# Three of the seven products of the last matrix product split once more, from the second block on

## The chip, the cores and the metric

The kernel runs on one core of one Trainium2 chip. The metric is device microseconds from start to end of one execution. The kernel before takes 3126.12 us (median of three runs, 3125.75 to 3136.84).

## What is computed

The input is x, 4 batches of 2048 tokens with 512 channels, fp32. With xn = layernorm(x) the result is

```
xr, xk, xv = mixes of xn and of xn one token earlier, weights mu_r, mu_k, mu_v
r, k, v    = xr Wr^T, xk Wk^T, xv Wv^T                      (512 -> 512 each)
wkv        = the RWKV-v4 recurrence over tokens, per channel, on k and v
attn       = (sigmoid(r) * wkv) Wo^T                        (512 -> 512)
hidden     = fwht(silu(xn W1^T) * (xn W3^T))                (512 -> 2048)
out        = x + attn + hidden W2^T                         (2048 -> 512)
```

fwht is a fixed orthogonal transform of the 2048 hidden channels; the kernel folds it into W2 once, at its start. The last two products are then one: 2048 hidden rows and 512 rows of sigmoid(r)*wkv, together 2560 rows, are multiplied by one matrix with 512 output columns.

## The kernel before, in words

All tensors have channels on the 128 partitions and tokens along the free dimension. The tokens are cut into 8 blocks of 1024 (`TB`), two to a batch. Every block passes through three stages.

1. **Projections** (k, v, r in this order). From block 1 on each is done by `projected_pair` (line 365), six units in all, `n` = 0 to 5.
2. **Up** (W1 and W3), 16 units of `up` (line 396). Between their instructions `step()` issues, piece by piece, the recurrence `wkv` on VectorE and ScalarE.
3. **Down**, the last product (`down`, line 496), 2560 rows into 512 columns. While it runs, the chores of the next block are issued (`next_tokens`, line 689): its tokens are loaded, their layernorm statistics taken (`statistics`, line 134), the input normalised (`normalize`, line 145), mixed (`mixed`) and combined (`mix_forms`).

All three stages use a scheme with seven instead of eight products (Strassen's, in Winograd's order). The right side (rows x 1024 tokens) is cut into four quarters: two halves of the rows and two halves of 512 tokens; the weights into four quarters alike. Sums of weight quarters are made once and kept in DRAM (`part_w` for projections and up, `down_w` for down), seven forms per weight. Sums of the right-hand quarters are made on VectorE or GpSimd as they are needed, and the seven products are added up partly in PSUM, partly by copies on ScalarE and additions on VectorE. In `down` one of the seven products is 10 row tiles (`NR`) for each of two groups `g` of 128 output channels: 20 matmuls of 128x128 weights by 512 tokens. Seven products are 140 matmuls. The right-hand quarters are named y11, y12, y21, y22 there; `difference` overwrites them in place as the products no longer need their old content.

**Order.** `InOrder` (line 24) keeps the instructions of every engine in the order in which the program issues them. All DMAs are issued by one queue, SyncE's (SP). An instruction there that waits (a store for the addition that fills its source, say) holds everything behind it.

**Weights.** Those of projections and up come in units of 896 KB through a ring of three buffers (`ring_a`, `load_parts`, line 349), two units ahead. The first two units of the next block are loaded by `next_parts` (line 709), which `down` calls as `w_after` ahead of its seventh product:

```
            if k == 6:
                w_after()
            elif k:
                w.append(load_down(i, order[k + 1]))
```

The weights of `down` come as whole forms of 1280 KB (`load_down`, line 483) into `ring_b`, two buffers. The four stage buffers (`stage`, line 96) and `x22_of` hold the residual x, take the sums, and are stored to `outT` from there. `x_tok` (the next block's tokens) lies in `k_sb`, whose content the recurrence has used up by then.

Of the kernel before, what the change touches and what calls it, by code (L numbers as in the profile page):

```python
# [14 lines left out]
P = 128  # L15
# [24 lines left out]
def tile_rwkv_attn_hadamard_ffn(  # L40
# [20 lines left out]
    NR = (NF + NB) // 2  # L61
    n_blocks = NT // TB
# [6 lines left out]
    ring_b = ctx.enter_context(tc.tile_pool(name="ring_b", bufs=2))  # L69
# [6 lines left out]
    down_w = dram.tile([7, P, NR, KH, P], F32, name="down_w")  # L76
# [3 lines left out]
    hid = const.tile([P, NF, TB], F32, name="hid")  # L80
    xnT = const.tile([P, NB, OFF + TB], F32, name="xnT")
    tf = const.tile([P, 4, KH, H], F32, name="tf")
    r_sb, k_sb, v_sb = (const.tile([P, NB, TB], F32, name=n) for n in ("r_sb", "k_sb", "v_sb"))
# [3 lines left out]
    turn = [0]  # L87

# [11 lines left out]
    mix_of[2], mix_of[0] = hid[:, 0:NB, :], hid[:, NB : 2 * NB, :]  # L100
    t4_of = {kind: hid[:, NF // 2 + n, :] for n, kind in enumerate((1, 2, 0))}
# [43 lines left out]
    def normalize():  # L145
        for b in range(NB):
            eng = dve if b < KH else pool
            for s, op in ((0, ALU.mult), (1, ALU.add)):
                xb = xnT[:, b, OFF : OFF + TB]
                eng.tensor_tensor(xb, xb, spread[:, s, :], op)  # L150
# [52 lines left out]
    def load_square(i, kind):  # L203
        t = ring_b.tile([P, NB, C], F32, tag="b", name=f"w_{i}_{kind}")
        sp.dma_start(out=t, in_=wrkv[kind])
        return t

    def projected(kind, w, h, half):
        pt = bank()
        for b in range(NB):  # L210
            pe.matmul(
                pt, lhsT=w[:, b, ts(h, P)], rhs=mix_of[kind][:, b, ts(half, H)], start=(b == 0), stop=(b == NB - 1)
            )
        dst = (r_sb, k_sb, v_sb)[kind][:, h, ts(half, H)]
        if kind == 0:
            act.activation(dst, pt, AF.Tanh, scale=0.5)
        else:
            act.copy(dst, pt)


    def wkv(h):
        w_h, u_h = weff[:, h : h + 1], vec[:, 4, h : h + 1]
        r, k, v = r_sb[:, h, :], k_sb[:, h, :], v_sb[:, h, :]
# [67 lines left out]
    def mix_forms(kind):  # L291

        m11, m12, m21, m22 = quarters(mix_of[kind], 0)
        if kind == 1:
            f1, f2 = (by_tile(s[:, OFF : OFF + TB]) for s in (sa, sb))
        else:
            slot = ring_b.tile([P, 2, KH, H], F32, tag="b", name=f"mf_{kind}")
            f1, f2 = slot[:, 0], slot[:, 1]
        f4 = by_tile(t4_of[kind])
        right_of[kind] = (m11, m21, m22, f1, f2, m12, f4)  # L300
        for out, x, y in ((f1, m12, m11), (f2, m22, f1), (m12, m22, m12), (f4, m21, f2)):
            dve.tensor_tensor(out, x, y, ALU.subtract)
            yield
# [61 lines left out]
    def projected_pair(i, n, w, tail, hook):  # L365
# [3 lines left out]
        dst = (r_sb, k_sb, v_sb)[kind]  # L369
        d11, d12, d21, d22 = (dst[:, mh * KH + g, ts(t, H)] for mh in range(2) for t in range(2))  # L370
# [25 lines left out]
    def up(i, j, w, tail, step):  # L396

        keep_parts(i, 3 * KH + j, w)
        h0, h1 = hid[:, j, 0:H], hid[:, j, H:TB]
# [24 lines left out]
    NP = NF // 2  # L424
    fold = [hid[:, NP + n, :] for n in range(NP)]

# [37 lines left out]
    def down_parts(n):  # L464
        t = ring_b.tile([P, 7, KH, P], F32, tag="b", name=f"df_{n}")
        if n >= NP:
            sp.dma_start(out=t[:, 0:4], in_=wo[n - NP])
        return t

    def down_forms(j, at, t):  # L470
        n, a = at[j] if j < NP else (j, None)
        far = down_w[:, :, n].rearrange("f p k c -> p f k c")
        if n < NP:
            a = a.rearrange("p (k m g c) -> p k m g c", k=2, m=2, c=P)
            seven_forms([t[:, f] for f in range(4)], a[:, 0, 0], a[:, 1, 0], a[:, 1, 1], a[:, 0, 1])
            sp.dma_start(out=far[:, 0], in_=a[:, 0, 0])
            sp.dma_start(out=far[:, 1:3], in_=a[:, 1])
            sp.dma_start(out=far[:, 3:7], in_=t[:, 0:4])
        else:
            forms_in(t)  # L480
            sp.dma_start(out=far, in_=t)

    def load_down(i, form):
        t = ring_b.tile([P, NR, KH, P], F32, tag="b", name=f"dw_{i}_{form}")
        sp.dma_start(out=t, in_=down_w[form])
        return t

    def rows(kh, half):

        n = NF // 2  # L490
        pieces = [hid[:, kh * n + 2 * a : kh * n + 2 * a + 2, ts(half, H)] for a in range(n // 2)]
        return pieces + [r_sb[:, kh * KH : (kh + 1) * KH, ts(half, H)]]

    order = (0, 1, 4, 6, 5, 3, 2)

    def down(i, w, between, w_after, last):
        y11, y12, y21, y22 = rows(0, 0), rows(0, 1), rows(1, 0), rows(1, 1)
        def product(k, pts, right, start, then):
            if k == 6:
                w_after()  # L500
            elif k:
                w.append(load_down(i, order[k + 1]))
            if k:
                next(between)
            for g in range(KH):
                whole = slice(0, H)
                for pt, cols in ending if last and k == 6 and g == KH - 1 else [(pts[g], whole)]:
                    for n in range(NR):
                        pe.matmul(
                            pt[:, cols], lhsT=w[k][:, n, g, :], rhs=right[n // 2][:, n % 2, cols],  # L510
                            start=start and n == 0, stop=n == NR - 1, skip_group_check=True,
                        )
                    then(g) if cols == whole else c21(g, pt, cols)

        def difference(out, x0, x1):
            for o, p0, p1 in zip(out, x0, x1):
                dve.tensor_tensor(o, p0, p1, ALU.subtract)

        def at(mh, g, half):
            return ts(mh * KH + g, P), ds(i * TB + half * H, H)  # L520

        def residual(slot, mh, g, half):
            c, t = at(mh, g, half)
            sp.dma_start(out=slot, in_=xT[c, t])

        def store(slot, mh, g, half):
            c, t = at(mh, g, half)
            sp.dma_start(out=outT[c, t], in_=slot)

        add = dve.tensor_tensor  # L530
        pa, pb, pc = ([bank() for _ in range(KH)] for _ in range(3))
        ending = [(pb[KH - 1], slice(0, H // 2)), (bank(), slice(H // 2, H))]
        s5 = [small.tile([P, H], F32, tag="s5", name=f"s5_{i}_d{g}") for g in range(KH)]
        for g in range(KH):
            residual(stage[g], 0, g, 0)
        product(0, pa, y11, True, lambda g: act.copy(pb[g], pa[g]))
        difference(y11, y12, y11)

        def c11(g):
            add(stage[g], pa[g], stage[g], ALU.add)  # L540
            store(stage[g], 0, g, 0)
            residual(stage[2 + g], 0, g, 1)
            residual(x22_of[g], 1, g, 1)

        product(1, pa, y21, False, c11)
        product(2, pc, y11, True, lambda g: act.copy(s5[g], pc[g]))
        difference(y12, y22, y12)
        for g in range(KH):
            add(x22_of[g], x22_of[g], s5[g], ALU.add)
        product(3, pc, y22, False, lambda g: None)  # L550
        difference(y22, y22, y11)

        def u2(g):
            act.copy(u2_of[g], pb[g])

        product(4, pb, y22, False, u2)
        difference(y21, y21, y22)
        for g in range(KH):
            add(u2_of[g], u2_of[g], stage[2 + g], ALU.add)
            add(stage[2 + g], pc[g], u2_of[g], ALU.add)  # L560
            store(stage[2 + g], 0, g, 1)
            residual(stage[g], 1, g, 0)

        def c22(g):
            add(x22_of[g], pb[g], x22_of[g], ALU.add)
            store(x22_of[g], 1, g, 1)
            if last and g == KH - 1:
                act.copy(ending[1][0][:, H // 2 :], pb[g][:, H // 2 :])

        product(5, pb, y12, False, c22)  # L570

        def c21(g, pt=None, cols=slice(0, H)):
            add(stage[g][:, cols], (pb[g] if pt is None else pt)[:, cols], stage[g][:, cols], ALU.add)
            c, t = at(1, g, 0)
            sp.dma_start(out=outT[c, t][:, cols], in_=stage[g][:, cols])

        product(6, pb, y21, False, c21)
# [29 lines left out]
    for i in range(n_blocks):  # L607
# [64 lines left out]
        w_down = []  # L672
        for j in range(NF):
# [6 lines left out]
            if j >= NF - 2:  # L680
                w_down.append(load_down(i, order[j - NF + 2]))
# [7 lines left out]
        def next_tokens():  # L689
# [4 lines left out]
            normalize()  # L694
            yield
            mixed(1)
            yield
            pending[1] = mix_forms(1)
            for _ in range(3):
                next(pending[1])  # L700
            yield
            yield
            mixed(2)
            pending[2] = mix_forms(2)
            for _ in range(3):
                next(pending[2])
            yield

        def next_parts():
            if not last:  # L710
                parts.extend(load_parts(i + 1, n) for n in range(2))
# [3 lines left out]
        down(i, w_down, (None for _ in range(6)) if last else next_tokens(), next_parts, last)  # L715
# [53 lines left out]
```

## Time and profile before

| | |
|---|---|
| profiled execution, its own time | 3126.89 us |
| its span, first to last instruction | 3125.1 us |
| TensorE matmul busy | 3108.2 us (99%), 7252 records |
| VectorE busy | 2197.2 us (70%) |
| ScalarE busy | 873.9 us (28%) |
| GpSimd busy | 322.6 us (10%) |
| mean granted TensorE clock | 0.999 |
| DMA | 334.45 MB, mean 107 GB/s |

An fp32 matmul is recorded as two matmuls, each with its weight load, so 7252 records are 3626 matmuls of the program. Block 3, as an example, has its projections from 1200 us, its up stage to 1463.3 us and its down stage from 1463.28 to 1583.45 us. The down stage's busy times there (1463 to 1583 us) are 120.0 us TensorE, 66.65 us VectorE, 12.02 us ScalarE and 13.70 us GpSimd.

### The profile page before, as it was taken

The numbers are of one execution on the slowest core, as the hardware profiler recorded it, in microseconds if no ns is written. First come the engines' busy times: TensorE is split into PE (matmuls) and PEld (weight loads), VectorE is DVE, ScalarE is ACT, GpSimd is POOL, SyncE is SP. The second block draws the span as 40 slices with busy tenths as digits, with TensorE's granted clock in tenths as the row PEclk, the third lists the DMA queues.
The fourth block names the chain that finished last, engine by engine and source line by source line (L and its number), as shares of the span: only waits on it lengthen the run. The fifth ranks groups of instructions, "written<-read, shape, count | busy, mean of one in ns | idle before, by whom it ended". The sixth has DMA issues, their size and how long they took to land.

```text
span 3125.1 us, 20283 instructions
## 1 busy us (share of the span) xinstructions
PE 3108.2 (99%) x7252; PEld 1378.9 (44%) x7252; DVE 2197.2 (70%) x2317; ACT 873.9 (28%) x1375; POOL 322.6 (10%) x203
## 2 busy tenths in 40 slices
PE   8999999999999999999999999999999999999999
PEld 3444444444444444444444444444444444444444
DVE  6798847876478765797557965589564886658852
ACT  4233023330233203332123321333213331133310
POOL 3353131001100011000110001100011000010000
PEclk9999999999999999999999999999999999999999
DMA  4354433223322242222422233222332224322222
GB/s 163 104 183 162 161 116 110 77 109 135 108 77 76 103 153 96 76 78 107 150 93 78 75 133 123 97 75 79 136 135 78 79 74 160 111 84 73 80 97 78
DMA packets 75813, 334.45 MB, mean 107 GB/s; under 512 B 9152, under 2 KB 18624, under 8 KB 66368
## 3 DMA queue, kind: packets, MB, share of 16 engines
q1 hardware_dynamic: 75712, 333.15, 30.3%
q8 instruction: 58, 0.95, 0.1%
q14 instruction: 43, 0.35, 0.0%
HBM read 286.93 MB, written 46.19 MB: 107 GB/s over the span
## 4 chain that ended last, share of the span: by engine, by line
PE 99%; DVE 0%; DMA 0%; SPq 0%; issue 0%; ACT 0%; ACTq 0%
PE bank L34 99%; DVE xnT L34 0%; DMA hid<-w 0%; DVE tf L34 0%; SPq L34 0%; ACT tf L34 0%; ACT hid L34 0%; DVE v_sb L34 0%; ACTq L34 0%; ACT k_sb L34 0%
## 5 line engine op out<-in xcount | busy, mean ns | idle before, releaser
L34 PE MATMUL bank<-tf,part 128*128 128x512 f32 x2272 | 1042.2, 592 | 0.0
L34 PE MATMUL bank<-hid,dw 128*128 128x512 f32 (+1 forms) x1808 | 787.5, 588 | 0.0
L34 PE MATMUL bank<-xnT,part 128*128 128x512 f32 x1536 | 721.8, 592 | 0.0
L34 PEld LDWEIGHTS bank<-tf,part 128*128 128x128 f32 x2272 | 431.7, 190 | 543.4 <-issue 513.5
L34 ACT COPY bank<-bank 128x512 f32<-128x512 f32 x527 | 300.2, 570 | 1268.1 <-PE bank L34 1243.9
L34 PEld LDWEIGHTS bank<-hid,dw 128*128 128x128 f32 x1808 | 343.5, 190 | 426.0 <-issue 422.8
L34 PEld LDWEIGHTS bank<-xnT,part 128*128 128x128 f32 x1536 | 291.8, 190 | 367.4 <-issue 363.1
L34 DVE TENSOR_TENSOR hid<-hid 128x1024 f32<-128x1024 f32 (+1 forms) x173 | 221.8, 1310 | 105.2 <-PE bank L34 104.3
L34 DVE SCALAR_TENSOR_TENSOR hid<-hid,bank 128x512 f32<-128x512 f32 x256 | 174.0, 680 | 170.8 <-ACT hid L34 170.6
L34 PE MATMUL bank<-hid,part 128*128 128x512 f32 x616 | 271.2, 592 | 0.0
L34 DVE RECIPROCAL e1b<-e1b 128x512 f32<-128x512 f32 x64 | 214.1, 3347 | 1.1
L34 PE MATMUL bank<-r_sb,dw 128*128 128x512 f32 (+1 forms) x452 | 210.7, 588 | 0.0
L34 DVE TENSOR_TENSOR bank<-bank,s 128x512 f32<-128x512 f32 x256 | 168.0, 690 | 36.5 <-ACT bank L34 25.3
L34 ACT ACTIVATE hid<-bank 128x512 f32<-128x512 f32 x272 | 162.2, 600 | 94.0 <-PE bank L34 75.9
L34 PEld LDWEIGHTS bank<-hid,part 128*128 128x128 f32 x616 | 117.0, 190 | 147.3 <-issue 145.7
L34 DVE TENSOR_TENSOR hid<-hid,bank 128x512 f32<-128x512 f32 x256 | 173.6, 678 | 11.5 <-PE bank L34 7.1
L34 POOL TENSOR_TENSOR rs<-rs,neg_half 128x8 f32<-128x8 f32 x7 | 11.5, 1648 | 1581.1 <-DVE rs L34 1581.1
L34 DVE SCALAR_TENSOR_TENSOR hid<-xnT,vec,hid 128x1024 f32<-128x1024 f32 x64 | 93.1, 1489 | 97.2 <-ACT hid L34 97.2
L34 PEld LDWEIGHTS bank<-r_sb,dw 128*128 128x128 f32 x452 | 85.9, 190 | 106.4 <-issue 106.2
L34 ACT COPY s<-bank 128x512 f32<-128x512 f32 x128 | 75.0, 586 | 145.9 <-PE bank L34 145.9
L34 DVE TENSOR_TENSOR v_sb<-bank,v_sb 128x512 f32<-128x512 f32 (+1 forms) x33 | 22.1, 672 | 129.9 <-PE bank L34 129.9
L34 POOL TENSOR_TENSOR tf<-xnT 128x1024 f32<-128x1024 f32 x16 | 46.4, 2902 | 589.9 <-PE bank L34 589.9
(103 smaller groups left out, 2218.0 us busy)
## 6 DMA issues: line engine op xcount, KB each, us to landing
part<-part_w SPq DMA_DIRECT2D x148, 896.0 KB, 4.6
dw<-down_w SPq DMA_DIRECT2D x56, 1280.0 KB, 6.1
part_w<-part SPq DMA_DIRECT2D x22, 896.0 KB, 6.9
k_sb<-x SPq DMA_DIRECT2D x7, 2048.0 KB, 8.3
xnT<-xT SPq DMA_DIRECT2D x7, 2048.0 KB, 9.7
v_sb<-xT SPq DMA_DIRECT2D x48, 256.0 KB, 4.8
out<-v_sb SPq DMA_DIRECT2D x47, 256.0 KB, 2.1
part<-wpart SPq DMA_DIRECT2D x22, 512.0 KB, 5.0
```

Source lines behind the costliest of these rows:

```text
L34: return self.tc.keep_in_program_order(issue(*args, **kwargs))
```

## The change

Block 0 keeps the 140 matmuls of its down stage. From block 1 on, the products with forms 1, 4 and 6 (on y21, y11 and y22) are each split once more by the same scheme: their 10 row tiles into two halves of 5 (`QR`), their two channel groups, and their 512 tokens into two halves of 256. Such a product becomes seven products of 5 matmuls by 256 tokens, 35 in place of 20 by 512 tokens. The other four products stay.

- **Weights in pieces.** `pieces_w` holds eight pieces of 5 x 128 x 128 (320 KB). Every product of 5 matmuls has its own piece, loaded by `load_piece` seven products ahead. The extra weight forms are made once, in block 1's up stage on GpSimd (`deep_forms`, `keep_deep`, DRAM tensor `deep_w`). `pieces_w` also takes the place of the former `ring_b`. `down_w` has a new layout.
- **Right side.** `hid` and `r_sb` become one tensor `right`, so that five row tiles lie at one stride. The sums for the deep products (`Deep.forms`) are made on VectorE; they lie in the three buffers of `ring_a`, in `k_sb` and in `tf`. Differences are made by quarters of 5 x 256 elements (`differences`, `parts_of`).
- **PSUM and output.** A deep product clears half banks (`clear`, ScalarE), copies half banks within itself (`step`, ScalarE), and its two banks are added into the stage buffers (`onto`, VectorE).
- **Chores.** `next_tokens` is cut into 23 steps, handed out by `advance(n)` at other places; `normalize` runs wholly on VectorE instead of half on GpSimd.
- **First units of the next block.** `load_parts(i + 1, 0)` and `(i + 1, 1)` are now issued after `down` has returned.

The core of the diff:

```diff
-    ring_b = ctx.enter_context(tc.tile_pool(name="ring_b", bufs=2))
-    hid = const.tile([P, NF, TB], F32, name="hid")
+    right = const.tile([P, 2, NR, TB], F32, name="right")
+    pieces_w = const.tile([P, 8, QR, P], F32, name="pieces_w")
     def normalize():
         for b in range(NB):
-            eng = dve if b < KH else pool
             for s, op in ((0, ALU.mult), (1, ALU.add)):
                 xb = xnT[:, b, OFF : OFF + TB]
-                eng.tensor_tensor(xb, xb, spread[:, s, :], op)
+                dve.tensor_tensor(xb, xb, spread[:, s, :], op)
+                yield
...
+    program = [p1[0], p1[1], *deep(0, 0, 1), p1[2], *deep(0, 2), p1[3], *deep(0, 3, 4, 5), *deep(1, 0), *deep(0, 6)]
+    for m, n in ((1, 1), (2, 0), (1, 2), (2, 1), (1, 3), (1, 4), (2, 2), (1, 5), (2, 3), (2, 4), (2, 5), (1, 6), (2, 6)):
+        program += deep(m, n)
+    program += plain(5) + plain(3) + plain(2)
+    def piece(i, u):
+        return pieces_w[:, (u + 4 - len(program if i else whole_program)) % 8]
...
+        def product(self, pt, rows, cols, start=False):
+            load_piece(self.i, self.u + 7)
+            self.u += 1
+            self.matmuls(pt, self.u - 1, rows, cols, start)
...
+    class Deep:
+        def forms(self, *which):
+            q11, q12, q21, q22 = self.q
+            t1, t2, t3, t4 = self.t
+            for n in which:
+                difference(*((t1, q12, q11), (t2, q22, t1), (t3, q22, q12), (t4, q21, t2))[n])
+        def step(self, *which):
+            for n in which:
+                pt, rows, cols = (
+                    (a, q11, lo), (f, t1, lo), (b, t2, hi), (a, q22, hi), (a, q21, lo), (b, t3, hi), (b, t4, lo),
+                )[n]
+                self.down.product(pt, rows, cols)
+                if n == 0:
+                    act.copy(b[:, hi], a[:, lo])
+                elif n == 1:
+                    act.copy(self.s5, f[:, lo])
+                elif n == 2:
+                    act.copy(a[:, hi], b[:, hi])
+                elif n == 5:
+                    act.copy(b[:, lo], b[:, hi])
...
+    def down(i, advance, last):
+        d0.forms(0, 1, 2, 3)
+        plain_step(0, 0)
+        plain_step(0, 1)
+        d1.clear()
+        add(x11[0], pa[0])
+        advance(1)
+        d0.step(0, 1)
+        plain_step(1, 0)
+        differences(y11[0:2], y12[0:2], y11[0:2])
+        d1.forms(0)
+        d0.step(2)
+        differences(y12[0:2], y22[0:2], y12[0:2])
+        plain_step(1, 1)
+        add(x11[1], pa[1])
+        differences(y11[2:4], y12[2:4], y11[2:4])
+        d1.forms(1)
+        d0.step(3, 4)
+        d0.onto(x11, 0)
+        d1.forms(2, 3)
+        d0.step(5)
+        d1.step(0)
+        d0.step(6)
+        differences(y12[2:4], y22[2:4], y12[2:4])
+        d2.forms(0)
+        d0.onto(x11, 1)
+        d2.clear()
+        d2.forms(1)
+        d1.step(1)
+        d2.step(0)
+        d2.forms(2, 3)
+        d1.step(2)
+        d2.step(1)
...
+        d.plain_product(pa, (1, 1), c12)
+        d.residual(x21, 1, 0)
+        differences(y21, y21, y22)
+        d.plain_product(pa, (0, 1), c22)
+        advance(7)
+        if not last:
+            d.plain_product(pa, (1, 0), c21)
+            return
...
-        def next_parts():
-            if not last:
-                parts.extend(load_parts(i + 1, n) for n in range(2))
-
         if not last:
             load_tokens(i + 1)
-        down(i, w_down, (None for _ in range(6)) if last else next_tokens(), next_parts, last)
+        if i == 0:
+            down_whole(i, advance)
+        else:
+            down(i, advance, last)
+        if not last:
+            parts.extend(load_parts(i + 1, n) for n in range(2))
```

`c21(g)` adds the last sum into a stage buffer and stores it to `outT`; it is called after each half of the last product.

## The prediction, made before the changed kernel had run

> **What bounds the kernel now.** I read the list of waits first: no engine's wait on TensorE (PE) matters if PE itself never waits. Then the chain that ended last, the groups by form for the price of a matmul, and the timeline around one block boundary. The chain:
>
> ```profile
> 8.86 5.58 PE bank L34 x8
> ...
> 21.73 17.43 PE bank L34 x36
> ...
> 45.20 3076.61 PE bank L34 x7188
> 3121.81 0.02 issue
> 3121.83 0.42 DVE v_sb L34
> ```
>
> From 45 us on the chain is PE alone: its matmuls stand back to back, across the block boundaries too. So only two things count: how long PE needs, and whether the change makes it wait.
>
> The price of a matmul of each width, from the timeline of the ending, where the old kernel already has 256 columns (two records are one fp32 matmul):
>
> ```profile
> 3113.00 3.62 PE L34 MATMUL bank<-hid,dw 128*128 128x256 f32 x16
> 3116.45 1.03 PE L34 MATMUL bank<-r_sb,dw 128*128 128x256 f32 x4
> 3117.31 3.62 PE L34 MATMUL bank<-hid,dw 128*128 128x256 f32 x16
> ```
>
> 20 records from 3113.00 to 3117.31 are 0.2155 us each, 0.431 us a matmul. Of 512 columns, the 280 records of block 3's down stage (1463.28 to 1583.45) are 0.4292 each, 0.858 a matmul. Half the width costs half the time, with a weight load (190 ns) for each record.
>
> The boundary between block 3 and 4, from the timeline:
>
> ```profile
> 1567.58 0.92 SPq L34 DMA_DIRECT2D part<-part_w  x2
> 1576.11 8.60 SPq L34 DMA_DIRECT2D out<-v_sb  x2
> 1583.45 1.88 PE L34 MATMUL bank<-tf,part 128*128 128x512 f32 x4
> 1583.65 0.69 DVE L34 TENSOR_TENSOR v_sb<-bank,v_sb 128x512 f32<-128x512 f32 x1 [7.57 <-PE bank L34]
> 1584.76 0.42 SPq L34 DMA_DIRECT2D part<-part_w  x1
> ```
>
> PE goes over to the next block at 1583.45 without a gap, because that block's first two weight units were issued at 1567.58, before the last two stores. Those stores held SP's queue for 8.6 us, until the addition that PE's last matmul released (1583.65).
>
> **1. Fewer PE microseconds.** A deep product is 35 x 0.431 = 15.09 us in place of 20 x 0.858 = 17.16. Three a block, seven blocks: 420 matmuls of 512 columns go (360.4 us), 735 of 256 come (316.8): **-43.6 us**, 6.2 a block. The end of the last block was in halves before, so nothing changes there.
>
> **2. The block's first weights, moved behind the last store.** In the changed program unit 0 of the next block is issued by SP after both stores of c21, and the next block's first matmul waits for it. From PE's last matmul at T: the addition starts at T+0.20, ends at T+0.89, and SP gets to the unit at T+1.31 (1584.76 - 1583.45). Units (896 KB) land 4.0 us after issue at the least, 4.6 as the median; the three that were issued as the first of two took 4.7 to 5.4. Here three go out in a row, so I take 5.0. The first wait in the trace went from landing (8.73) to matmul in 0.14. PE idles 1.31 + 5.0 + 0.14 = **6.4 us** (5.4 to 6.9). Unit 1 lands some 2 us later and is needed 12 us later. Block 1's first units are the 512 KB kind, landing in 5.0, whose forms GpSimd makes at 0.99 each while PE has raw quarters: the same gap.
>
> An idle PE also loses its clock. At 17.86 us it stopped for 3.87 us:
>
> ```profile
> 14.27 3.60 PE L34 MATMUL bank<-hid,had_sb 128*128 128x512 f32 x8
> 21.73 12.26 PE L34 MATMUL bank<-tf,w 128*128 128x512 f32 x24 [3.87 <-ACT hid L34]
> ```
>
> The next PE row starts at 33.83: 24 records took 12.10 us, at 0.429 they are 10.30. The stop cost **1.8 us** more, and single records between 23.3 and 25 us show 1061 ns against 592. I take 1.8 for a gap of 6.4 us as well; the ends are 0 (the stop of 0.86 us at 44.3 shows no slow records) and 3.6, twice the row, since the gap is longer.
>
> The Trainium skill ("TensorE: Matmul & The Clock Gate", Part 1) states that an idle window of 3.4 us halves the clock until a busy window has passed, the windows running free. By that rule I estimate one to two half-speed windows, 1.7 to 3.4 us a boundary, and an end of 3139 to 3151.
>
> Seven boundaries: 7 x (6.4 + 1.8) = **+57.4 us**. What hid these loads before is the whole seventh product, 17 us; the change keeps no cover.
>
> **3. VectorE (DVE) in the down stage.** Rows: 1024 elements in a run of subtractions 4.62/4 = 1.155 us, so a quarter of 1280 is 1.44; an addition from PSUM 0.69, of 256 columns 0.43. With t from the stage's first matmul, DVE is free at 2.2 (1465.5 - 1463.28, its last up additions). The four d0 sums end at 8.0; the first addition follows PE's tenth matmul, 8.8 to 9.5; the statistics take 7.5 as before (1481.81 to 1489.3, GpSimd's power in them) and end at 17.2. Then DVE is solid work: 3 quarters and 2 of y12 to 24.6, an addition to 25.3, 3 quarters to 29.6, d0's first output (1.15) to 30.8, 5 quarters (d1's last two sums, two of y12, d2's first sum) to 38.0. PE wants d1's first operand at 30.1 (ready 18.9), d1's second sum at 38.7 (ready 29.6), d2's first sum at 40.9 (ready 38.0), y22 at 62.4 (ready 57.6, behind PE's reading), y21 at 96.7 (ready 86.3). Smallest slack **2.8 us**: nothing on the path. The added work, 12 sums (17 us) and about 6 us of additions a block, fits: DVE was busy 66.65 of 120 us there. Block 0 keeps its products; its y22 quarters are ready 1.2 us ahead.
>
> Normalising on DVE: the 1024-element rows are 1.22 alone and 2.98 while GpSimd works beside it. Three such steps at 49.9 and five at 64 leave y22 in time even at 2.98 (ready 61.7). They cost nothing; if DVE were late, each would cost its length.
>
> **4. Weights in pieces.** 37 of 320 KB for 7 of 1280: 2.9 MB more a block. The stage moved 125 GB/s; 406 GB/s was reached within it. Each piece is asked for seven products ahead, 15 us in the deep stretch, except where SP stands: the statistics' write goes out at 17.2, the broadcast at 19.2 (2.04 later, as at 1489.34 and 1491.38), and piece 9 only then, at 19.6. PE wants it at 27.9. Transfers issued 0.9 to 1.3 us behind that broadcast landed in:
>
> ```profile
> DMA to landing us min/median/max: 5.6/5.7/5.8
> ```
>
> So at about 25.4, with 2.5 us to spare; the pieces behind it follow closer than PE eats them (2.16 us each). Nothing on the path. Worst row: 10.1 us (a 2 MB load), late by 1.8, six blocks, 11 us.
>
> **5. The rest.** ScalarE's half-bank copies (0.36 us) stand one other product (2.16) before their use, clears long before; it was 10% busy in the stage. GpSimd's 12 sums for the deep weights, once, are at most 12 x 2.5 us (994 ns for 256 elements) beside an up stage in which GpSimd was idle; they slow DVE by at most what its rows show (1.91 against 1.22), within its 28 spare us of 178. The smaller rows of the new `down_w` lengthen block 0's stores at a DMA share of 0.47. All zero; bound together 0 to 5 us.
>
> **The sum.** The profiled execution took 3126.89 (span 3125.1): 3126.89 - 43.6 + 57.4 = 3140.7. The median is 0.8 lower: **3140 us**, 0.4% slower. A measurement of this kernel tells about 0.5%, some 16 us, from no change.
>
> **Rivals.**
> *Gap hidden:* if the units landed in time, 3126 - 44 = 3082. For it: the ring's buffers are free 50 us before the end. Against: SP's order, which the 8.60 us row shows to hold what is behind. 0.09.
> *Gap without clock loss:* 3126 - 43.6 + 7 x 6.4 = 3127. For it: 1.8 us rests on one stop. Against: that stop was shorter. 0.13.
> *A piece late (slower):* piece 9 behind statistics and broadcast, 3140 + 11 = 3151. It decides once landing takes over 8.3 us. The rows near it say 5.7; but 2 MB of tokens and pieces go beside it. 0.15.
> *DVE as the bound (slower):* it decides when a quarter takes over 1.65 us (2.8 us over 13 of them); at 1.91 for 1024 elements, 2.39 a quarter, PE waits 9.4 us a block, 3200. That row had GpSimd beside it, which is idle here. 0.08.
>
> **The numbers.** My case has 0.55; with the clock loss from 0.8 to 3 it spreads from 3131 to 3150, two fifths of it above 3141.8, the 0.5% bound. Faster: 0.09, rounded up to 0.1. Slower: 0.15 + 0.08 + 0.22 = 0.45. Same: 0.13 + 0.33, 0.45. The range 3121 to 3160 leaves out the hidden gap and most of the DVE case; its lower end is a gap of 5.4 us without clock loss (3120), its upper a late piece and the dearest clock.
>
> **What would show it.** Seven waits of PE for `part` of about 6.4 us each, at the boundaries; slow records after each; 7882 matmul records; a down stage of 114 us from block 1 on, without gaps; `part` issued right after the last store. I am wrong if PE waits for `pieces_w`, `right` or `k_sb`, or if no gap stands at the boundary.

## The result: slower by 0.8%, in the upper part of the range

The changed kernel takes 3154.16 us (median of four runs, 3152.08 to 3156.34) against 3125.93 us (3124.66 to 3136.84) for the kernel before on the same chip: a ratio of 1.0083, 95% interval 1.0059 to 1.0106. The prediction was 3140 (3121 to 3160). The profiled execution has a span of 3152.8 us, 27.7 more than before, with 3085.7 us of matmuls in 7882 records and a mean granted clock of 0.991.

The waits of TensorE (PE) in the kernel after; the columns are the total in us, how often, and the longest:

```profile
PE bank L34 <- DMA part<-part_w: 38.5, 6, 6.8
PE bank L34 <- DMA part<-wpart: 10.4, 3, 4.9
...
PE bank L34 <- DVE bank L34: 2.0, 1, 2.0
...
PE bank L34 <- POOL part L34: 0.5, 1, 0.5
```

The first line and one entry of the second (4.9) are the seven block boundaries. The other two of `wpart` and the last two lines are new, and none of them was in the forecast. The chain that ended last (start, length, what) shows where they lie:

```profile
44.42 161.67 PE bank L34 x376
...
237.10 6.65 DMA part<-wpart
...
252.12 6.36 DMA part<-wpart
...
258.64 2.35 POOL part L34
...
261.03 178.81 PE bank L34 x416
...
440.97 3.71 DMA part<-wpart
...
444.72 380.34 PE bank L34 x986
...
826.18 5.54 DMA part<-part_w
...
831.86 381.53 PE bank L34 x986
...
1214.52 5.48 DMA part<-part_w
...
1220.13 380.25 PE bank L34 x986
```

Before, PE was one unbroken step from 45.20 us. Now a weight load stands in the chain at each boundary (three are shown; 6.06 to 6.82 us of idle each, 4.89 at the first), and twice in block 0's up stage, at 237.10 and 252.12.

The boundary between block 3 and 4, from the timeline of the kernel after:

```profile
1592.88 8.59 SPq L34 DMA_DIRECT2D out<-v_sb  x2
...
1600.41 0.69 DVE L34 TENSOR_TENSOR v_sb<-bank,v_sb 128x512 f32<-128x512 f32 x1 [7.56 <-PE bank L34]
...
1601.52 1.38 SPq L34 DMA_DIRECT2D part<-part_w  x3
...
1606.74 3.75 PE L34 MATMUL bank<-tf,part 128*128 128x512 f32 x4 [6.37 <-DMA part<-part_w]
...
1610.29 3.02 PE L34 MATMUL bank<-sa,part 128*128 128x512 f32 x4
...
1613.15 1.88 PE L34 MATMUL bank<-sb,part 128*128 128x512 f32 x4
```

The stores hold SP's queue, the addition that PE's last matmul releases ends at 1601.10, and only then, at 1601.52, `part` is asked for. PE stands 6.37 us. Then its clock is low: in the stretch from 1606.74 to 1613.15 us the profile grants TensorE 0.54 of full speed, and the rows of four records are 3.75 and 3.02 us long, and 1.88 from 1613.15 on. The eight records from 1606.74 to 1613.15 took 6.41 us; at 0.429 they are 3.43. So 2.98 us are lost here on top of the gap.

The down stage of block 3, from the windows (length of the stretch; busy us and instructions of PE, weight load, VectorE, ScalarE, GpSimd; granted clock, DMA share, GB/s):

```profile
1486.00:1600.00 114.00, 114.00 (x371) 70.12 (x369) 86.39 (x95) 15.03 (x27) 1.64 (x1) 1.00 0.41 132
```

PE is busy through the whole window at full clock. The stage runs from 1486.22 us to PE's last record at 1600.37, 114 us, 6 less than before. VectorE rose from 66.65 to 86.39 us and held nobody up.

**Where the 27.7 us come from.** Fewer matmul microseconds -43.6 (by the forecast's prices, which e5_whole below bears out). Seven idle boundaries +43.4 (4.89, 6.82, 6.75, 6.37, 6.22, 6.25, 6.06). The slow records behind them +16.8 (1.81, 3.00, 1.73, 2.98, 1.98, 3.15, 2.15; each counted like the one above). Block 0's up stage +10.8 (from the start of PE's long run at 44.42 us to the boundary with block 1 it is 395.4 us; before, from 45.20 to the row below, block 1's first matmuls, 384.6). The start -0.8 (44.42 for 45.20). Together +26.6; 1.1 us are left. Most of that is the way of counting: idle time is counted from the end of a record (0.59 us after its start in the profile), while an undisturbed PE starts a record every 0.429 us, so each gap costs 0.16 us more than its idle, 1.1 at seven gaps.

```profile
429.85 1.88 PE L34 MATMUL bank<-tf,part 128*128 128x512 f32 x4
```

So the forecast missed by 14 us, mainly in two places: the clock (16.8 for 12.6) and block 0 (10.8 for nothing); the idle at the boundaries was 1.4 less than forecast. The four new waits of PE in block 0, from the timeline of the kernel after:

```profile
226.94 1.96 PE L34 MATMUL bank<-xnT,part 128*128 128x512 f32 x4 [1.98 <-DVE bank L34]
...
243.88 3.62 PE L34 MATMUL bank<-xnT,part 128*128 128x512 f32 x4 [4.69 <-DMA part<-wpart]
...
258.62 1.95 PE L34 MATMUL bank<-xnT,part 128*128 128x512 f32 x4 [0.81 <-DMA part<-wpart]
261.03 1.55 PE L34 MATMUL bank<-tf,part 128*128 128x512 f32 x3 [0.46 <-POOL part L34]
```

What is issued there, in the program's order: for each of the first ten up units `down_forms` sums the weights of one row tile on GpSimd and stores the sums into `down_w`; behind the store, on the same queue, `load_parts` asks for a later unit's weights (`wpart`); GpSimd makes that unit's forms when they have landed, and then the sums of the next store. So a late store makes a late unit, and that a late store. (The first of the four waits is put down to VectorE here and to `wpart` in e1_early; it goes with the others below.) SyncE's queue and GpSimd in the kernel after:

```profile
236.64 0.37 SPq L34 DMA_DIRECT2D down_w<-pieces_w  x1
237.10 0.65 SPq L34 DMA_DIRECT2D part<-wpart  x1
...
251.66 0.37 SPq L34 DMA_DIRECT2D down_w<-pieces_w  x1
252.12 1.18 SPq L34 DMA_DIRECT2D part<-wpart  x1
```

```profile
243.87 4.79 POOL L34 TENSOR_TENSOR part<-part 128x256 f32<-128x256 f32 x4 [7.26 <-issue]
248.62 3.01 POOL L34 TENSOR_TENSOR pieces_w<-pieces_w 128x256 f32<-128x256 f32 x4
```

Load issued 237.10, landed for GpSimd at 243.87, forms to 248.66, sums to 251.63, store 251.66, next load 252.12: a round of 15.0 us, while PE uses up a unit in 12.0 us. The kernel before had this loop too, with the ninth of these loads at 223.31 us instead of 237.10. Two things differ in it: its first sums start at 106.32 us instead of 114.32, and the rows it stores into `down_w` are 1 KB instead of 512 B. Two rows of the kernel before, from the timelines of GpSimd and of SyncE's queue:

```profile
106.32 1.18 POOL L34 TENSOR_TENSOR df<-e 128x256 f32<-128x256 f32 x1 [26.62 <-issue]
```

```profile
223.31 0.51 SPq L34 DMA_DIRECT2D part<-wpart  x1
```

The first difference comes from a buffer: the kernel after stages the first row tile in half 0 of `pieces_w`, where the weights of block 0's r product still lie, and GpSimd waits for PE to have read them:

```profile
114.32 0.72 POOL L34 TENSOR_TENSOR pieces_w<-e 128x256 f32<-128x256 f32 x1 [35.38 <-PE bank L34]
```

### The profile page after: what moved, and what is told of

It is laid out like the page before. It is cut to its first block, busy times and chain, and to the rows that moved or that the text cites. A ratio compares the mean times of both kernels' runs of the same rounds, so it can differ in the third digit from the quotient of the medians.

```text
span 3152.8 us, 22434 instructions
## 1 busy us (share of the span) xinstructions
PE 3085.7 (98%) x7882; PEld 1504.6 (48%) x7882; DVE 2336.2 (74%) x2481; ACT 894.7 (28%) x1459; POOL 263.4 (8%) x187
## 4 chain that ended last, share of the span: by engine, by line
PE 97%; DMA 2%; DVE 1%; SPq 0%; issue 0%; ACT 0%; POOL 0%; POOLq 0%; DVEq 0%; ACTq 0%
PE bank L34 97%; DMA part<-part_w 1%; DMA part<-wpart 1%; DVE e1b L34 0%; DMA xnT<-xT 0%; DVE xnT L34 0%; DVE v_sb L34 0%; SPq L34 0%; DVE right L34 0%; DVE tf L34 0%; DVE sb L34 0%; POOL part L34 0%; DVE bank L34 0%; ACT right L34 0%; ACT tf L34 0%
## 5 line engine op out<-in xcount | busy, mean ns | idle before, releaser
L34 PE MATMUL bank<-right,pieces_w 128*128 128x512 f32 (+1 forms) x2598 | 888.6, 503 | 0.0
L34 ACT COPY bank<-bank 128x512 f32<-128x512 f32 (+1 forms) x576 | 314.7, 546 | 1546.9 <-PE bank L34 1505.6
L34 PEld LDWEIGHTS bank<-right,pieces_w 128*128 128x128 f32 x2598 | 493.7, 190 | 389.2 <-issue 356.1
L34 DVE TENSOR_TENSOR right<-right 128x1280 f32<-128x1280 f32 (+2 forms) x201 | 288.7, 1469 | 27.7 <-PE bank L34 26.7
L34 DVE SCALAR_TENSOR_TENSOR right<-right,bank 128x512 f32<-128x512 f32 x256 | 173.8, 679 | 175.3 <-ACT right L34 175.1
L34 PE MATMUL bank<-right,part 128*128 128x512 f32 x616 | 271.2, 592 | 0.0
L34 ACT ACTIVATE right<-bank 128x512 f32<-128x512 f32 x308 | 183.9, 600 | 121.3 <-PE bank L34 102.8
L34 PEld LDWEIGHTS bank<-right,part 128*128 128x128 f32 x616 | 117.1, 190 | 147.3 <-issue 145.6
L34 DVE TENSOR_TENSOR right<-right,bank 128x512 f32<-128x512 f32 x256 | 173.4, 677 | 11.5 <-PE bank L34 7.1
L34 POOL TENSOR_TENSOR part<-part 128x256 f32<-128x256 f32 x88 | 95.3, 1094 | 189.5 <-DMA part<-wpart 156.6
```

What stands on the lines that cost most here:

```text
L34: return self.tc.keep_in_program_order(issue(*args, **kwargs))
```

## The experiments

Theories ahead of the runs. *Boundary:* seven gaps with their slow records cost about 60 us, and SP's order alone causes them. *Block 0, buffer:* the wrong half makes the loop late; the rival is the smaller rows, which lengthen its stores. Each run was timed beside the kernel before; the ratio is to that.

**The next block's units asked for earlier (e1_early).** `load_parts(i + 1, 0)` and `(i + 1, 1)` go out ahead of the last product, as in the kernel before.

```diff
         if not last:
+            next_parts()
             d.plain_product(pa, (1, 0), c21)
...
-        if not last:
-            parts.extend(load_parts(i + 1, n) for n in range(2))
```

(in `down`, and the same in `down_whole`)

> The changed kernel (3154.2 us) with the next block's first two weight units issued ahead of the down stage's last product, after c22's stores, as the old kernel had it. Theory (order on SP): PE's seven waits for part, 43.4 us, go, and with them the slow records behind each, 16.8 us: 3154.2 - 60.2 = 3094 us. Rival (transfer): the units land late because the queue's many small pieces and stores hold the DMA engines at the end of a block, wherever the issue stands; then at least half of the waits stay, above 3120 us.

Measured 3092.86 us, ratio 0.9882 (0.9866 to 0.9898). No boundary wait is left, and the chain runs unbroken from block 0's up stage on:

```profile
236.58 6.64 DMA part<-wpart
...
251.60 6.45 DMA part<-wpart
...
258.21 2.26 POOL part L34
...
260.52 2827.37 PE bank L34 x7338
```

61.3 us came back; the count from the trace gave 43.4 + 16.8 = 60.2, and 1.1 for the ends of the records. Block 0's waits stayed (1.80, 4.71, 0.91, 0.38 us).

**The same place, another queue (e4_queue).** The two loads stay behind the stores in the program, but ScalarE issues them.

```diff
-            parts.extend(load_parts(i + 1, n) for n in range(2))
+            parts.extend(load_parts(i + 1, n, act) for n in range(2))
```

> The changed kernel with the two loads at the same place of the program, after down, but issued by ScalarE's queue instead of SP's. ScalarE's last work ahead of them is the mix for v, done 12 us before the block's end. Theory (order on SP, not the place in the program): the gaps go as in the first run, 3094 us. Rival (the place in the program or the transfer itself): the gaps stay, 3150 us or more.

Measured 3093.46, ratio 0.9885 (0.9866 to 0.9904), without a boundary wait. The transfers themselves were always possible; the order on one queue held them. The Trainium skill ("DMA: Bandwidth & Descriptors", Rules for kernel authors) says that spreading DMAs over engines only saves issue time, since all use the same transfer engines. Here it saved 60.7 us, because an instruction that waits on one queue does not hold those on another; the rule is about bandwidth and is silent on that.

**The move alone, in the kernel before (e6_late).** Nothing else of the change:

```diff
-        down(i, w_down, (None for _ in range(6)) if last else next_tokens(), next_parts, last)
+        down(i, w_down, (None for _ in range(6)) if last else next_tokens(), lambda: None, last)
+        next_parts()
```

> The kernel before, with only the call that loads the next block's first two units moved from ahead of the seventh product to after the down stage. Theory (order on SP alone makes the gap): seven gaps of about 6.2 us and 2.4 us of slow clock behind each, 60 us: 3186 us. Rival (the gap needs the changed kernel's pieces and many small DMAs on SP): less than half of that, under 3156 us.

Measured 3183.87, ratio 1.0184 (1.0169 to 1.0199): about +57, the sum that step 2 of the prediction had. The waits of PE:

```profile
PE bank L34 <- DMA part<-part_w: 35.6, 6, 6.0
...
PE bank L34 <- DMA part<-wpart: 5.1, 1, 5.1
```

40.7 us of idle. The slow records behind the seven gaps, counted over eight records as above, cost 1.88 to 2.02 us each, 13.6 in all. With 1.1 for the ends of the records that is 55.4 of the 55.7 us by which the span of the profiled execution grew.

**PE kept busy in the gap (e9_warm).** Behind the last product stand 7 matmuls (5 after block 0) into a bank that nobody reads; they add no part of the result.

```diff
             d.plain_product(pa, (1, 0), c21)
+            for n in range(7):
+                pe.matmul(sets[1][2], lhsT=had_sb, rhs=xnT[:, 0, OFF : OFF + H], start=True, stop=True)
```

> The changed kernel (gaps at the boundaries as they are) with 7 matmuls of no use after each down stage (5 after block 0's), 6.0 us of work in the gap that writes a bank that nobody reads. Theory (the slow records behind the gap come from PE's idleness): the 16.8 us of slow clock at the boundaries go and the wait itself stays covered by these matmuls: 3154.2 - 16.8 = 3137 us. Rival (the slow records come from the wait for the DMA or from the first matmuls of a block): 3150 us or more.

Measured 3137.95, ratio 1.0028 (1.0017 to 1.0039): 16.2 us less than the kernel after, where the slow records were counted as 16.8. The units come as late as before, but the block starts at full speed. The timeline of this run, block 2 to 3:

```profile
1207.63 6.17 PE L34 MATMUL bank<-xnT,had_sb 128*128 128x512 f32 x14
1213.92 1.96 PE L34 MATMUL bank<-tf,part 128*128 128x512 f32 x4
1215.71 1.88 PE L34 MATMUL bank<-sa,part 128*128 128x512 f32 x4
```

Four records take 1.96 us, against 3.75 behind an idle gap, and from 1213.92 to 1217.43 us the profile grants 1.00 of full speed, where it granted 0.54 behind the gap above. So PE's idleness makes the slow period, not the late weights or the DMA traffic.

**The buffer half (e2_ring), and both edits (e3_both).** The staging starts in the other half; e3_both is this and e1_early's edit.

```diff
     def down_parts(n):
-        t = half_ring(n, 7, KH, P)
+        t = half_ring(n + 1, 7, KH, P)
```

> The changed kernel with only the parity of the staging buffer for block 0's weight sums turned (n + 1 in place of n), so that the first of them falls into the half of pieces_w that the v weights leave, not the one that the r weights still hold. Theory (wrong half): GpSimd's first sum starts 8 us earlier, block 0's four waits (7.9 us) and the slow clock behind them (2.8 us) go: 3143.5 us. Rival (smaller rows): the 512-byte rows of the new down_w make block 0's stores slow, the loop of store, unit load and sums stays too long whatever its start: within 3 us of 3154.

> Both edits together. Theories of the two runs above: they add up, 3154.2 - 60.2 - 10.8 = 3083 us, 1.4% under the kernel before, no wait of PE over 1 us after 50 us. Rival: with PE never waiting, the down stage's VectorE chain or a piece behind the statistics becomes late (slack 2.8 and 2.5 us by the prediction), PE waits for right, k_sb or pieces_w in each block: above 3095 us.

Measured 3151.24 (1.0066, 1.0047 to 1.0086) and 3090.6 (0.9875, 0.9858 to 0.9892). In e2_ring GpSimd's first sum went forward as meant, to 105.16 us, but PE still waits:

```profile
225.03 1.95 PE L34 MATMUL bank<-xnT,part 128*128 128x512 f32 x4 [0.46 <-DMA part<-wpart]
...
241.83 3.75 PE L34 MATMUL bank<-xnT,part 128*128 128x512 f32 x4 [4.55 <-DMA part<-wpart]
...
257.75 1.95 PE L34 MATMUL bank<-xnT,part 128*128 128x512 f32 x4 [1.18 <-DMA part<-wpart]
```

2 to 3 us came instead of 11: the buffer alone was not it, and e3_both missed the 3083 us expected of it. My theory of block 0 fell. Left were the smaller rows, or the loop's order itself.

**1 KB rows (e7_rows), and the loop's order (e8_act0).** Both stand on e3_both. The first lays `down_w` out so that both channel groups of a row lie together; the second lets ScalarE issue block 0's unit loads, past the stores.

```diff
-    down_w = dram.tile([2, 7, KH, P, QR, P], F32, name="down_w")
+    down_w = dram.tile([2, 7, P, QR, KH, P], F32, name="down_w")
```

```diff
     def load_parts(i, n):
+        queue = act if i == 0 and n >= 3 * KH + 2 else sp
...
-            sp.dma_start(out=t[:, 0:4], in_=wpart[n])
+            queue.dma_start(out=t[:, 0:4], in_=wpart[n])
```

> The kernel with both edits, which still has about 6 us of PE waits in block 0, with down_w laid out so that its stores write rows of 1 KB as in the old kernel (the pieces are then read in rows of 512 bytes). Theory (small rows): the stores of 512-byte rows slow the unit loads behind them; with 1 KB block 0's waits go, 3083 us. Rival (order and sums): the loop of store, unit load and GpSimd's two sets of sums is too long by its order and by the length of the sums; within 2 us of 3090.6, and the waits in block 0 stay.

> The kernel with both edits, with block 0's unit loads from the third on issued by ScalarE's queue, so that they no longer stand behind the stores that wait for GpSimd's sums. Theory (order and sums): block 0's waits of PE, 6 us and the slow clock behind them, go: 3083 us. Rival (small rows, or GpSimd's sums alone too long): PE still waits for part in block 0, above 3088 us.

Measured 3083.45 (0.9863, 0.9842 to 0.9885) and 3083.85 (0.9857, 0.9841 to 0.9874). Both times came out as expected, and neither profile has a wait in block 0; the chain of e7_rows, with e8_act0's of the same length and count from 45.80 us:

```profile
44.55 3033.39 PE bank L34 x7818
```

One of e7_rows' four runs took 3092.84 us, as long as e10_rows_start below, in which PE waits in block 0; only the run of 3082.91 has a trace. So the 1 KB rows leave the loop near its edge. e8_act0's four runs lie between 3082.51 and 3084.82.

In e8_act0 the loads go out at the pace at which PE frees the buffers, every 12.0 us, from the timeline of ScalarE's queue:

```profile
202.39 0.33 ACTq L34 DMA_DIRECT2D part<-wpart  x1
...
214.40 0.33 ACTq L34 DMA_DIRECT2D part<-wpart  x1
...
226.42 0.33 ACTq L34 DMA_DIRECT2D part<-wpart  x1
```

**Each of these with the old half (e10_rows_start, e11_act0_start).** Without `half_ring(n + 1, …)`; the boundary edit stays.

> The kernel with early units and 1 KB rows, but with the old parity of the staging buffer: GpSimd's first sum for the last product's weights again waits for the r projection, 8 us later. Theory (rows alone): the late start never reaches PE once each turn of the loop is short enough, 3083 to 3085 us, no wait of PE for part in block 0. Rival (both count): the loop starts 8 us late with some 2 us to spare, so PE waits in block 0 again, some 3 to 8 us with the slow clock: 3087 to 3092 us.

> The kernel with early units and block 0's unit loads on ScalarE's queue, but with the old parity of the staging buffer (and 512-byte rows). Theory (order): the loads no longer wait for the sums, so the late start and the rows cost nothing, 3083 to 3085 us. Rival: the late start alone costs PE some us, 3087 us or more.

Measured 3092.8 (0.989, 0.9873 to 0.9906) and 3084.57 (0.9864, 0.9849 to 0.9879). In e10_rows_start the theory (rows alone) fell and its rival held: PE waits 6.3 us for `wpart` in block 0. In e11_act0_start the theory held: no wait there. The table has the six versions in which the units at the boundary come early. Its mean round is the time from the first to the ninth of the unit loads that follow a store in the program, divided by eight (on ScalarE's queue no store stands ahead of them):

| first sums | unit loads, rows of `down_w` | time | first and ninth load | mean round |
|---|---|---|---|---|
| 114 us (e1) | SP, 512 B | 3092.9 | 117.40, 236.58 | 14.9 |
| 106 us (e3) | SP, 512 B | 3090.6 | 110.95, 235.96 | 15.6 |
| 116 us (e10) | SP, 1 KB | 3092.8 | 119.00, 237.30 | 14.8 |
| 106 us (e7) | SP, 1 KB | 3083.5 | 110.72, 224.90 | 14.3 |
| 118 us (e11) | ScalarE, 512 B | 3084.6 | 120.22, 216.39 | 12.0 |
| 107 us (e8) | ScalarE, 512 B | 3083.9 | 118.24, 214.40 | 12.0 |

The kernel before has 111.34, 223.31 and 14.0. Its round was longer than PE's 12.0 as well: it lived on its head start, and a tenth load at 241.42 was in time for 249.6. Either the late start (e10) or the small rows (e3) uses the head start up, each alone. With ScalarE's queue neither the late start (e11) nor the small rows (e8) matters. So the order, a unit load behind a store that waits for GpSimd, is the root, and the change took its spare away twice. What stays open is why the small rows lengthen the round only with the early start (15.6 against 14.3, but 14.9 against 14.8 with the late one): their own transfer is little longer (512 KB stores 3.5 us in place of 3.2, but 3.2 with small rows too in e8, 3.7 in e11; the unit loads behind them 5.5 in the kernel after and 5.2 in e3, 4.8 in e7), and GpSimd's own sums vary by more than that. The kernel before has some runs 10 us longer than the rest as well (3136.84 above); none of them has a trace, so whether its loop falls behind in these is open.

**What the deep products are worth (e5_whole).** On both edits, only the last block's down stage splits deep; blocks 1 to 6 keep their 140 matmuls.

```diff
-        if i == 0:
-            down_whole(i, advance)
-        else:
-            down(i, advance, last)
         if not last:
-            parts.extend(load_parts(i + 1, n) for n in range(2))
+            down_whole(i, advance, next_parts)
+        else:
+            down(i, advance, last, next_parts)
```

> The kernel with both edits (turned buffer half, early units), in which blocks 1 to 6 keep the 140 matmuls of block 0's down stage and only the last block splits three products once more. Theory (matmul price): six blocks give back 6.24 us each, 37.4 us above the kernel with both edits: 3083 + 37 = 3120 us, close to the kernel before with its 3126 less one block's 6.2. Rival (the split costs more than its matmuls, in small waits for copies and sums): the difference is clearly under 37 us, 25 or less.

Measured 3126.21, ratio 0.9994 (0.9983 to 1.0006): 35.6 above e3_both. Its ten runs spread from 3122.62 to 3130.93, so the traces tell it more sharply. Without block 0's differing waits, from the point where both are unbroken, e5_whole and then e3_both:

```profile
255.47 2864.42 PE bank L34 x6798
```

```profile
260.75 2827.37 PE bank L34 x7338
```

37.05 us for 18 deep products, 2.06 each, where 20 x 0.858 - 35 x 0.431 gives 2.07. The saving is real and whole.

## Why the prediction was right, and where it was not

The mechanism and its sign held; the range held the time at its upper part. That the range held the time is in part luck: without the 10.8 us of block 0, which it had at zero, the time would have been near 3143, and the room above was kept for a late piece and a dearer clock. It gave slower and same 0.45 each; by its own bound of 0.5% the change is slower. By its own steps:

1. **Fewer matmul microseconds: right.** -43.6 was forecast, 2.07 a deep product; e5_whole gives 2.06, and the down stage takes 114 us as forecast.
2. **The moved weights: idle right, clock too small.** Forecast 6.4 us seven times, 44.8; measured 43.4. SP asked 1.11 us after the addition began, as worked out; landing, by the chain, took 4.8 to 5.5 us, and 3.7 at the first boundary. The mis-sized term is the clock: 1.8 a boundary from one stop of 3.87 us, measured 1.7 to 3.15, mean 2.4, within the ends of 0 and 3.6 that were stated. (The spread of 3131 to 3150 for a loss of 0.8 to 3 is 3133 to 3148 by the sum's own terms.) e1, e4 and e6 show the cause, e9 the clock's share.
3. **VectorE fits: right.** With t counted from the stage's first matmul, d2's first sum was forecast ready at t = 38.0, and PE wants it at 40.9. The kernel after's down stage starts at 1486.22; the row that ends with that sum:

```profile
1519.61 4.29 DVE L34 TENSOR_TENSOR right<-right 128x1280 f32<-128x1280 f32 x3
```

The sum is ready at 1523.9, t = 37.7. A quarter took 1.47 us (mean over the rows of the stage) where 1.44 was forecast, a normalising step 1.20. No wait of PE for `right` in the stage, for `pieces_w` or for `k_sb`.

4. **Pieces in time: right.** The broadcast went at t = 18.5 (19.2 forecast), the piece behind it at 18.9 (19.6), from SP's timeline:

```profile
1503.15 0.37 SPq L34 DMA_DIRECT2D stat_d<-rs  x1
1504.72 0.33 SPq L34 DMA_DIRECT2D v_sb<-stat_d  x1
1505.14 26.82 SPq L34 DMA_DIRECT2D pieces_w<-deep_w  x16
```

5. **"The rest", zero: the step that failed.** It named the smaller rows of block 0's stores and let a DMA share of 0.47 cover them; their cover was the loop's head start, not bandwidth. The buffer in which the staging begins was not listed at all. Measured 10.8 us, over the 5 allowed: 7.9 of waits, some 2.0 of slow records and 0.8 for the ends of records at the gaps. The runs e7, e8, e10 and e11 show the cause.

The rivals: *gap hidden* and *gap without clock loss* fell by the seven waits and by e9; *a late piece* and *VectorE as the bound* by the down stage without a gap. The time lies near the late piece's 3151, but from another place. The versions without the moved loads and without waits in block 0 (e7_rows, e8_act0) take 3083.5 to 3083.9 us, 1.4% less than the kernel before: the matmuls' saving, whole.

## What to carry to other kernels

On a queue that keeps order, price a load by the instruction ahead of it that waits, not by its bytes: here a load after a waiting store cost its whole latency at every block, and a second queue gave all of it back. Where a loop runs through two engines and a queue, compare its round with the pace of the engine that it feeds; a kernel without a wait may be living on a head start, and an edit that touches its first buffer or its row size spends it. Count an idle TensorE at the gap plus the slow records behind it (here 1.7 to 3.15 us behind gaps of 4.9 to 6.8).

## What the runs showed of the hardware that I had not expected

Behind idle gaps of 4.9 to 6.8 us in the kernel after the slow period cost 1.7 to 2.2 us four times and 3.0 to 3.15 three times, with no order by the length of the gap: 6.82 cost 3.00, 6.75 cost 1.73. These are not two fixed prices: e2_ring's seven gaps (5.0 to 6.5 us) cost 1.69 to 3.05, with 2.19, 2.41 and 2.87 between, and e6_late's seven (5.1 to 6.0 us) 1.88 to 2.02. The Trainium skill ("TensorE: Matmul & The Clock Gate", Part 1) says that the clock halves after an idle window of about 3.4 us, that the windows run free, and that the point of change therefore depends on where in a window the first matmul lands. The sizes agree with the estimate of 1.7 to 3.4 us worked out from it; that the place in the window is what spreads them is only argued.

GpSimd's sums of 256 elements have no fixed price: in the rows above four of them took 3.01 us and the four just ahead of them 4.79. So the loop through GpSimd has no steady round: the loads of block 0 in the kernel after follow each other after 12.3 to 17.0 us.
